# A decoder layer on one core: the first feed-forward turns one gate earlier, the last roots and the fifth weights later

## The chip, the cores and the metric

The kernel runs on one core of a Trainium2 chip. Time is the device time of that core in microseconds; lower is better. A run's time is that of the whole execution; the profile gives, for one profiled execution, the time of every instruction on the five engines: TensorE (PE; its weight loads are PEld), VectorE (DVE), ScalarE (ACT), GpSimd (POOL) and SyncE (SP), which issues most of the DMAs. All data is fp32.

## The reference

Four sequences (B = 4) of 1024 tokens with 512 features go through an attention, a gated convolution over pairs of neighbours, and a quantised feed-forward, each followed by a residual sum and a layer norm:

```python
x = layernorm(x + attention(x))            # 32 heads of 16
x = layernorm(x + xattn(x, ctx, fside))
x = layernorm(x + ffn(x))

def xattn(z1ss, uss, z0, weight, bias):    # h_size 512, kernel 2
    z1h, z1c = z1ss[:, :512], z1ss[:, 512:]
    z0c = concatenate([z0[:, 512:], z1c], axis=2)[:, :, :-1]
    conv = conv1d(concatenate([z0[:, :512], z1h], axis=2), weight)
    it, ot, gt, ft = split(uss + conv + bias, 4, axis=1)
    ct = sigmoid(ft) * z0c + sigmoid(it) * tanh(gt)
    ht = sigmoid(ot) * tanh(ct)
    return concatenate([ht, ct], axis=1)

def ffn(x, ternary_weight, bias, act_scale):
    x_int = clip(round(x / scale), -127, 127)
    return (x_int * scale) @ (ternary_weight - 1).T + bias
```

The convolution's channel axis is the token axis of the layer: rows 0 to 511 of a sequence give `ht` and rows 512 to 1023 give `ct`.

## The kernel before

The attention fills the first 1951 us or so and is not touched. The change lies in `tail`, which does the rest of the layer in two rounds (n = 0 for batches 0 and 2, n = 1 for batches 1 and 3). A round has these stages:

- In round 1 only, the output projection of both batches (`project_out`, lines 772 to 776), eight token tiles each, and the first norm of each batch (`first_norm`, 778 to 785).
- The gates: for each of four blocks t of 128 channels, for each batch of the round, for each of four gates g, one call of `gate` (792 to 819). It does two halves of 16 matmul records (four matmuls for each of two taps): the "ends" into one PSUM tile (`pc`), then the "mids" into another (`pa`). VectorE then adds both to the context with four instructions (lines 806, 809, 810, 812), and ScalarE applies a sigmoid or tanh (813). Both PSUM pools hold two tiles. The taps come from `xf`, which `fir_parts` makes on VectorE from the first norm's output (185 to 191).
- After the fourth gate of a block, `combine` (821 to 858) forms the new state: products on GpSimd (828 to 830), a tanh on ScalarE and sums on GpSimd (833 to 836), statistics on VectorE (841 and 107), the root on ScalarE (117, `deviations`), its reciprocal and the normalisation on VectorE (118 and 121), and a sum on GpSimd (855).
- The feed-forward (`feed_forward`, 914 to 954) over 16 tiles of 128 tokens: `quantise` (864 to 871: one pass on ScalarE, L868, and two on VectorE, L869 and L870), `turn` (873 to 879: four transposes on TensorE, L876, and a copy on ScalarE, L878), `feed` (881 to 885: matmuls, L884), `residual` (887 to 890), and the third norm in groups (`third_norm`, 892 to 908), whose last step, `finish`, writes the tile out.

The order of the tiles in the feed-forward is `order` = 0, 1, 2, 4, 5, 6, 3, 7: tiles 3 and 7 come out of the last block and go last. Tile k + 1 is turned ahead of the matmuls of tile k, and tile k + 3 is quantised behind them.

The program sets the order of instructions by hand (`manual_schedule`): each engine runs its own instructions in the order in which the Python code emits them. `after(n, work)` puts work off by n calls of `step`, one of which follows each gate, each projected tile and each fed tile. So a due number says behind which gate or tile an instruction is emitted, on every engine at once. An instruction that waits holds up all that was emitted behind it on its engine.

Line 983 turns tiles 0 and 1 of the round's first batch between the two halves of the very last gate, and line 987 quantises tiles 0, 1 and 2 in the three gates ahead of it (g = 0, 1, 2 of the second batch at t = 3). The convolution's weights are loaded one block ahead (`load_conv`, 156 to 166, four DMAs of 512 KB; even blocks share one buffer, odd ones another) and their taps summed on GpSimd by `sum_taps` (168 to 170), two instructions each. The weights of the fifth block (m = 4, the first of round 1) are loaded at t = 3 of round 0 (line 989), and summed ahead of the projection (line 969), emitted right behind the feed-forward.

```python
if t == 3 and b == batches[1] and g < 3:
    quantise(batches[0], order[g])
if b == batches[0] and g == 0 and (n, t) != (1, 3):
    w_next = hand.load_conv(4 * n + t + 1, wp)
```

Of the kernel before, what the change touches and what calls it, by code (L numbers as in the profile page):

```python
# [14 lines left out]
P = 128  # L15
B, S, D = 4, 1024, 512
# [3 lines left out]
NT = S // P  # L20
# [718 lines left out]
def tail(ctx, tc, a, out, ident, eps, hand):  # L739
    nc = tc.nc  # L740
# [37 lines left out]
    def first_norm(b):  # L778

        x1[b], parts = hand.first_norm(b)  # L780
        firs[b], more = hand.fir_parts(b, x1[b], hand.shared if b < 2 else fir)
        parts[0]()
        parts[1]()
        for n, part in zip((1, 1, 2, 3, 4, 5) if b == 1 else (1, 1, 2, 2, 3, 3), parts[2:] + more):
            after(n, part)


# [4 lines left out]
    def gate(b, t, g, w, between=None):  # L792
        xf, u = firs[b], us[b, t]
        o = g * P
        ends = ps_c.tile([P, 2, 256], F32, tag="c", name=f"pc{b}_{t}_{g}")
        mids = ps_a.tile([P, 2, 256], F32, tag="a", name=f"pa{b}_{t}_{g}")
        for tap in range(4):
            if tap == 2 and between:
                between()
            pt = (ends, mids)[tap // 2][:, tap % 2, 0:TR]  # L800
            for i in range(FT):
                nc.tensor.matmul(pt, w[:, i, tap, o : o + P], xf[:, tap, i, :], start=i == 0, stop=i == FT - 1)  # L802

        ug = u[:, g, :].rearrange("p (m e) -> p e m", e=3)
        outer = ug[:, 0:3:2, :]
        nc.vector.tensor_add(outer, ends[:, :, 0:TR], outer)
        m, n = (mids[:, i, 0:TR] for i in range(2))
        both = n.unsqueeze(1).to_broadcast([P, 2, TR])
        nc.vector.scalar_tensor_tensor(outer, both, 0.5, outer, ALU.mult, ALU.add)
        nc.vector.scalar_tensor_tensor(ug[:, 1, :], n, -0.5, ug[:, 1, :], ALU.mult, ALU.add)  # L810
        all3 = m.unsqueeze(1).to_broadcast([P, 3, TR])
        nc.vector.scalar_tensor_tensor(ug, all3, 0.5, ug, ALU.mult, ALU.add)  # L812
        nc.scalar.activation(  # L813
            u[:, g, 0:D],
            u[:, g, 0:D],
            AF.Tanh if g == 2 else AF.Sigmoid,
            bias=b_c[:, 4 * g + t : 4 * g + t + 1],
            scale=1.0,
        )

    def combine(b, t, k):


        u, y, x = us[b, t], ys2[b], x1[b]
        ig, og, gg, fg = (u[:, i, 0:D] for i in range(4))
        both = (t, 4 + t)
        made = []
        nc.gpsimd.tensor_mul(gg, ig, gg)
        nc.gpsimd.tensor_mul(fg, fg, x[:, 4 + t, 0:D])
        nc.gpsimd.tensor_add(fg, fg, gg)  # L830

        def second():
            nc.scalar.activation(ig, fg, AF.Tanh)
            nc.gpsimd.tensor_add(y[:, 4 + t, :], fg, x[:, 4 + t, 1 : D + 1])
            nc.gpsimd.tensor_mul(og, og, ig)
            nc.gpsimd.tensor_add(y[:, t, :], og, x[:, t, 1 : D + 1])
            hand.load_ctx(k + 2)

        def third():
            for n, tt in enumerate(both):  # L840
                nc.vector.bn_stats(stats2[b][:, 2 * t + n, :], y[:, tt, :])
            made.append(hand.means(stats2[b], stat, f"2_{b}", 2 * t, 2))

        def fourth():
            made.extend(hand.deviations(made[0], stat, f"2_{b}", 2 * t, 2))

        def fifth():
            mv, rstd, invert = made
            invert()
            for n, tt in enumerate(both):  # L850
                hand.normalised(y[:, tt, :], y[:, tt, :], mv, rstd, 2 * t + n)

        def sixth():
            for tt in both:
                nc.gpsimd.tensor_add(x[:, tt, 0:D], y[:, tt, :], b_f)

        for n, work in ((1, second), (3, third), (4, fourth), (5, fifth), (6, sixth)):
            after(n, work)


# [31 lines left out]
    def third_norm(b, n0, n):  # L892

        y = ys2[b]
        made = []

        def first():
            for m in range(n0, n0 + n):
                halves = 2 if (b, m) == (B - 1, NT - 1) else 1
                nc.vector.bn_aggr(mv3[b][:, m, :], stats3[b][:, m : m + halves, :].rearrange("p h c -> p (h c)"))  # L900
            made.extend(hand.deviations(mv3[b], stat, f"3_{b}", n0, n))

        def finish(m):
            t = order[m]
            hand.normalised(y[:, t, :], y[:, t, :], mv3[b], made[0], m)
            nc.sync.dma_start(out[b, t * P : (t + 1) * P, :], y[:, t, :])

        return first, lambda: made[1](), [lambda m=m: finish(m) for m in range(n0, n0 + n)]

# [2 lines left out]
    mv3 = {}  # L912

    def feed_forward(batches):

        tiles = [(b, n, order[n]) for b in batches for n in range(NT)]
        for b in batches:
            stats3[b] = stat.tile([P, NT + 1, 6], F32, tag="stats3", name=f"stats3_{b}")
            mv3[b] = stat.tile([P, NT, 2], F32, tag="mv3", name=f"mv3_{b}")
        closing = []  # L920
        for k, (b, n, t) in enumerate(tiles):
            end = len(tiles) - k
            if 0 < k < len(tiles) - 1:
                turn(tiles[k + 1][0], tiles[k + 1][2])
            if (b, n) == (B - 1, NT - 1):

                for half in range(2):
                    cols = slice(half * 256, half * 256 + 256)
                    pt = feed(b, t, cols)
                    residual(b, n, t, pt, cols, half)  # L930
            else:
                pt = feed(b, t)
                if k + 3 < len(tiles):
                    quantise(tiles[k + 3][0], tiles[k + 3][2])
                residual(b, n, t, pt)
            for work in closing:
                work()
            closing = []

            last = b == batches[1]  # L940
            group = {5: 2, 6: 1, 7: 1}.get(n, 4 if n == 3 else 0) if last else 4 * (n % 4 == 3)
            if group:
                first, invert, parts = third_norm(b, n + 1 - group, group)
                first()
                if group == 4:
                    after(1, invert)
                    for m, part in enumerate(parts):
                        after(1 + m, part)
                elif group == 2:
                    closing = [invert] + parts  # L950
                else:
                    for work in [invert] + parts:
                        work()
            step()
# [11 lines left out]
    for n, batches in enumerate(((0, 2), (1, 3))):  # L966
        if n:
            for i in range(FT):
                hand.sum_taps(w_next, i)
            for b in batches:  # L970
                if b == 3:
                    after(2, lambda: first_norm(1))
                project_out(b, range(NT))
            first_norm(3)
        for b in batches:
            ys2[b] = hand.tokens(b, f"y2_{b}")
            stats2[b] = stat.tile([P, NT, 6], F32, tag="stats2", name=f"stats2_{b}")
        for t in range(4):
            w = w_next
            for b in batches:  # L980
                for g in range(4):
                    last = (b, t, g) == (batches[1], 3, 3)
                    gate(b, t, g, w, (lambda: [turn(batches[0], order[m]) for m in (0, 1)]) if last else None)
                    if g == 3:
                        combine(b, t, k)
                    if t == 3 and b == batches[1] and g < 3:
                        quantise(batches[0], order[g])
                    if b == batches[0] and g == 0 and (n, t) != (1, 3):
                        w_next = hand.load_conv(4 * n + t + 1, wp)
                        if t < 3:  # L990
                            for i, m in enumerate((3, 6, 6, 7)):
                                after(m, lambda w=w_next, i=i: hand.sum_taps(w, i))
                    step()
                k += 1
        if n == 0:
            big3 = lambda: hand.shared.tile([P, NT * (D + 1)], F32, tag="big0", name="big3")
            after(9, lambda: hand.load_attention(3, big3()))
            after(13, lambda: hand.load_residual(1))
            after(18, lambda: hand.load_residual(3))
        feed_forward(batches)  # L1000
    while later:
        step()

# [40 lines left out]
```

## Time and profile before

| | us |
|---|---|
| runs (3): median, lowest, highest | 2454.65, 2454.08, 2454.93 |
| the profiled execution | 2454.71 |
| its span | 2452.9 |
| TensorE busy | 2431.9 |
| VectorE busy | 1736.9 |
| ScalarE busy | 1337.4 |
| GpSimd busy | 373.7 |
| round 0: gates, feed-forward | from 1951.1, from 2105.2 |
| round 1: projection, gates, feed-forward | from 2171.9, from 2226.9, from 2382.2 |

A row of the timeline gives start, duration, engine, line, operation, output and input with their sizes, and how many instructions are merged (x8 is eight records; a matmul of fp32 data leaves two). In brackets stands how long the engine was idle before it and what ended that. A line of the waits gives who waited for whom, the total, the number of waits and the longest. A row of windows gives the stretch, its length, the busy time, the clock granted to TensorE (1.00 is full speed), the DMA engines' share and GB/s.

### The profile page before, as it was taken

Reading aid. Unit: us, or ns where it says so; the run is one execution under the profiler, and the core shown is the slowest. Engines: PE = TensorE matmul, PEld = TensorE weight load, DVE = VectorE, ACT = ScalarE, POOL = GpSimd, SP = SyncE. Lnnn points to the kernel's source line nnn. Section 1 sums busy time; section 2 is a strip of 40 time slices with the busy share of each in tenths; the row PEclk is TensorE's granted clock in tenths of the full one; section 3 lists DMA queues with packets and bytes.
Section 4 is the critical chain, followed back from the end, with each engine's and each line's share of the span. In section 5 each row is a group of like instructions: output and inputs, shape, how many; then the busy total and the mean of one; then the engine's idle time right before and its main releaser. Section 6 shows DMA issues by size and latency. Waiting matters only on the chain.

```text
span 2452.9 us, 74387 instructions
## 1 busy us (share of the span) xinstructions
PE 2431.9 (99%) x32604; PEld 1691.8 (69%) x32604; DVE 1736.9 (71%) x2180; ACT 1337.4 (55%) x2592; POOL 373.7 (15%) x310
## 2 busy tenths in 40 slices
PE   9999999999999999999999999999999999999998
PEld 5566666666666666666666666666666699548984
DVE  3777777777777777777777777777777476868667
ACT  1166666666666666666666666666655623311332
POOL 2000000000000000000000001000020276502760
PEclk9999999999999999999999999999999999999999
DMA  6101112111111211111111114110120243150311
GB/s 220 50 12 21 21 23 58 22 21 25 22 25 21 53 23 26 21 21 21 21 26 21 22 23 130 26 27 19 25 80 12 85 160 121 52 189 18 121 35 69
DMA packets 80708, 121.70 MB, mean 50 GB/s; under 512 B 39056, under 2 KB 39056, under 8 KB 80384
## 3 DMA queue, kind: packets, MB, share of 16 engines
q1 hardware_dynamic: 79808, 115.90, 16.8%
q8 instruction: 256, 4.19, 0.7%
q10 hardware_dynamic: 576, 1.05, 0.1%
q14 instruction: 68, 0.56, 0.1%
HBM read 80.77 MB, written 18.35 MB: 40 GB/s over the span
## 4 chain that ended last, share of the span: by engine, by line
PE 97%; DVE 2%; ACT 1%; issue 0%; DVEq 0%
PE nat L457 22%; PE av L553 20%; PE st L527 18%; PE proj L59 10%; PE pa L802 5%; PE pc L802 5%; PE v L59 5%; PE pf L884 4%; PE po L59 2%; PE po L237 2%; PE fold L361 1%; PE fold L59 1%; PE tr L876 0%; DVE xq L869 0%; DVE y L121 0%; DVE xq L870 0%
## 5 line engine op out<-in xcount | busy, mean ns | idle before, releaser
L473 DVE TENSOR_REDUCE mx<-nat 128x2 f32<-128x1024 f32 x1008 | 1187.7, 1219 | 439.7 <-PE st L527 412.1
L538 ACT ACTIVATE at<-st 128x512 f32<-128x512 f32 x2016 | 1042.3, 603 | 608.1 <-PE st L527 595.6
L457 PE MATMUL nat<-qk 32*128 32x512 f32 x4032 | 1012.2, 614 | 0.5 <-DVE mx L473 0.5
L527 PE MATMUL st<-qk 32*128 32x256 f32 x8064 | 998.0, 387 | 0.0
L527 PEld LDWEIGHTS st<-qk 32*128 32x128 f32 x8064 | 662.2, 184 | 46.1 <-issue 3.7
L553 PE MATMUL av<-at,v_sb 128*32 128x256 f32 x8192 | 498.5, 382 | 1.5 <-ACT at L538 1.5
L457 PEld LDWEIGHTS nat<-qk 32*128 32x128 f32 x4032 | 343.2, 184 | 188.3 <-DVE mx L473 119.7
L553 PEld LDWEIGHTS av<-at,v_sb 128*32 128x32 f32 x8192 | 241.0, 109 | 223.6 <-ACT at L538 92.3
L600 POOL TENSOR_TENSOR o_n<-o_sb,rbc 128x512 f32<-128x512 f32 x64 | 98.1, 1555 | 1673.2 <-DMA rbc<-rec_d 1619.1
L59 PE MATMUL proj<-xT,w_qk 128*32 128x176 f32 (+1 forms) x6144 | 259.4, 311 | 0.7 <-ACT w_qk L366 0.7
L59 PEld LDWEIGHTS proj<-xT,w_qk 128*32 128x32 f32 x6144 | 181.3, 109 | 82.0 <-ACT at L538 60.0
L802 PE MATMUL pc<-xf,w 128*128 128x171 f32 x1024 | 160.0, 308 | 1.6 <-DVE xf L191 1.0
L802 PE MATMUL pa<-xf,w 128*128 128x171 f32 x1024 | 159.8, 308 | 0.0
L802 PEld LDWEIGHTS pc<-xf,w 128*128 128x128 f32 x1024 | 152.0, 189 | 2.8 <-DVE xf L191 1.2
L802 PEld LDWEIGHTS pa<-xf,w 128*128 128x128 f32 x1024 | 152.0, 189 | 0.0
L813 ACT ACTIVATE u<-u,b_c 128x512 f32<-128x512 f32 x64 | 46.3, 723 | 163.6 <-DVE u L812 163.6
L884 PE MATMUL pf<-w_f,xq_t 128*128 128x512 f32 (+1 forms) x264 | 120.8, 604 | 7.6 <-ACT xq_t L878 7.6
L59 PE MATMUL v<-w_v,xT 128*32 128x256 f32 x2048 | 122.5, 382 | 0.0
L566 DVE TENSOR_TENSOR o_sb<-av,o_sb 128x256 f32<-128x256 f32 x128 | 54.3, 424 | 72.0 <-PE av L553 71.4
L59 PEld LDWEIGHTS v<-w_v,xT 128*32 128x32 f32 x2048 | 60.6, 109 | 58.1 <-ACT at L538 16.6
L170 POOL TENSOR_TENSOR w<-w 128x512 f32<-128x512 f32 x64 | 80.5, 1292 | 110.5 <-DMA w<-in_conv_wT 110.5
L564 ACT COPY o_sb<-av 128x256 f32<-128x256 f32 x128 | 48.0, 375 | 77.9 <-PE av L553 59.3
(99 smaller groups left out, 1321.7 us busy)
## 6 DMA issues: line engine op xcount, KB each, us to landing
qk<-qk SPq DMA_DIRECT2D x256, 64.0 KB
w<-in_conv_wT SPq DMA_DIRECT2D x32, 512.0 KB
u<-in_ctx SPq DMA_DIRECT2D x16, 1024.0 KB
xT<-in_xT SPq DMA_DIRECT2D x16, 512.0 KB
rbc<-rec_d SPq DMA_DIRECT2D x128, 64.0 KB
attn<-o_n SPq DMA_DIRECT2D x256, 32.0 KB
big<-attn SPq DMA_DIRECT2D x4, 2048.0 KB
y<-in_x SPq DMA_DIRECT2D x4, 2048.0 KB
```

Of the source, the lines that this page charges most:

```text
L59: nc.tensor.matmul(pt[r, :], lhsT(f)[:, r], rhs(f), start=f == 0, stop=f == FT - 1)
L170: self.nc.gpsimd.tensor_tensor(w[:, i, tap, :], w[:, i, 0, :], w[:, i, 1, :], op)
L237: nc.tensor.matmul(pt, attn_t[:, f, t * P : (t + 1) * P], self.w_o[:, f, cols], start=f == 0, stop=f == FT - 1)
L457: nc.tensor.matmul(pts[n], q_ts[u % 4][r : r + 32, qt * P : (qt + 1) * P], k_ts[u % 4][r : r + 32, kh * 512 : kh * 512 + 512], start=True, ...
L473: nc.vector.tensor_reduce(mxs[u][:, qt, 2 * pair : 2 * pair + 2, kh], pt, AX.X, ALU.max, negate=True)
L527: nc.tensor.matmul(st[:, k * QW : k * QW + QW], k_ts[u % 4][r : r + 32, kt * P : (kt + 1) * P], q_ts[u % 4][r : r + 32, qq * QW : qq * QW ...
L538: nc.scalar.activation(at, st, AF.Exp, scale=0.25)
L553: nc.tensor.matmul(av[32 * j : 32 * j + 32, :], v_sb[b % 2][:, kt, c * VW : c * VW + 32], ats[u, 2 * i + n // 2, j][:, n % 2 * QW : n % 2 ...
L566: nc.vector.tensor_add(o, av, o)
L600: nc.gpsimd.tensor_mul(o_n[:, :, half * 256 : half * 256 + 256], o_sb[:, cols].rearrange("p (s e) -> p e s", e=2), rbc[:, cols].rearrange( ...
L802: nc.tensor.matmul(pt, w[:, i, tap, o : o + P], xf[:, tap, i, :], start=i == 0, stop=i == FT - 1)
L884: nc.tensor.matmul(pt, xq_ts[b, t][:, f, :], hand.w_f[:, f, cols], start=f == 0, stop=f == FT - 1)
```

## The change

Five things are done.

- `quantise` of tiles 0, 1, 2 moves one gate earlier: to the last gate of the first batch and the first two of the second ("place" 3, 4, 5). The turn of tiles 0 and 1 moves from the last gate to the one ahead of it ("place" 6), again between its halves.
- `combine`'s root, normalisation and bias sum of the last block (t = 3) are due two steps later.
- In the feed-forward, a group's first step (its aggregate and root) is emitted ahead of what the group before has left over, and the very last tile is normalised and written in two halves, the second DMA from ScalarE's queue.
- `first_norm` emits the two parts of the FIR (the making of `xf`) ahead of the normalisation of tiles 4 to 7, which `xf` does not read.
- The fifth block's weights are loaded behind the first feed-forward (behind its output DMAs on SP's queue), and their taps summed in the projection, at steps 3 to 6.

The diff, cut to what matters:

```diff
@@ first_norm
-        for n, part in zip((1, 1, 2, 3, 4, 5) if b == 1 else (1, 1, 2, 2, 3, 3), parts[2:] + more):
+        for n, part in zip((1, 1, 2, 3, 4, 5) if b == 1 else (1, 1, 2, 3, 4, 4), parts[2:4] + more + parts[4:]):
             after(n, part)
@@ combine
-        for n, work in ((1, second), (3, third), (4, fourth), (5, fifth), (6, sixth)):
+        late = 2 * (t == 3)
+        for n, work in ((1, second), (3, third), (4 + late, fourth), (5 + late, fifth), (6 + late, sixth)):
             after(n, work)
@@ third_norm
         def finish(m):
             t = order[m]
-            hand.normalised(y[:, t, :], y[:, t, :], mv3[b], made[0], m)
-            nc.sync.dma_start(out[b, t * P : (t + 1) * P, :], y[:, t, :])
+            n = 2 if (b, m) == (B - 1, NT - 1) else 1
+            for h in range(n):
+                part = y[:, t, h * D // n : (h + 1) * D // n]
+                hand.normalised(part, part, mv3[b], made[0], m)
+                (nc.scalar if h else nc.sync).dma_start(
+                    out[b, t * P : (t + 1) * P, h * D // n : (h + 1) * D // n], part
+                )
@@ feed_forward
-            for work in closing:
-                work()
-            closing = []
...
                 first()
+            for work in closing:
+                work()
+            closing = []
+            if group:
@@ tail
         if n:
             for i in range(FT):
-                hand.sum_taps(w_next, i)
+                after(3 + i, lambda i=i: hand.sum_taps(w_next, i))
...
                 for g in range(4):
-                    last = (b, t, g) == (batches[1], 3, 3)
-                    gate(b, t, g, w, (lambda: [turn(batches[0], order[m]) for m in (0, 1)]) if last else None)
+                    place = 4 * (b == batches[1]) + g if t == 3 else 0
+                    gate(b, t, g, w, (lambda: [turn(batches[0], order[m]) for m in (0, 1)]) if place == 6 else None)
                     if g == 3:
                         combine(b, t, k)
-                    if t == 3 and b == batches[1] and g < 3:
-                        quantise(batches[0], order[g])
-                    if b == batches[0] and g == 0 and (n, t) != (1, 3):
+                    if place in (3, 4, 5):
+                        quantise(batches[0], order[place - 3])
+                    if b == batches[0] and g == 0 and t < 3:
                         w_next = hand.load_conv(4 * n + t + 1, wp)
...
         feed_forward(batches)
+        w_next = hand.load_conv(4, wp) if n == 0 else None
```

No arithmetic is added or left out. Each round has two fewer loads of ScalarE's function table, since the root of batch 0's or 1's last block no longer stands between two sigmoids.

More of the change, by code (lines that the diff above doesn't have):

```diff
@@ L981, in tail @@
                 for g in range(4):
-                    last = (b, t, g) == (batches[1], 3, 3)
-                    gate(b, t, g, w, (lambda: [turn(batches[0], order[m]) for m in (0, 1)]) if last else None)
+                    place = 4 * (b == batches[1]) + g if t == 3 else 0
+                    gate(b, t, g, w, (lambda: [turn(batches[0], order[m]) for m in (0, 1)]) if place == 6 else None)
                     if g == 3:
                         combine(b, t, k)
-                    if t == 3 and b == batches[1] and g < 3:
-                        quantise(batches[0], order[g])
-                    if b == batches[0] and g == 0 and (n, t) != (1, 3):
+                    if place in (3, 4, 5):
+                        quantise(batches[0], order[place - 3])
+                    if b == batches[0] and g == 0 and t < 3:
                         w_next = hand.load_conv(4 * n + t + 1, wp)
-                        if t < 3:
-                            for i, m in enumerate((3, 6, 6, 7)):
-                                after(m, lambda w=w_next, i=i: hand.sum_taps(w, i))
+                        for i, m in enumerate((3, 6, 6, 7)):
+                            after(m, lambda w=w_next, i=i: hand.sum_taps(w, i))
                     step()
```

## The prediction, made before the changed kernel was run

> **What bounds the kernel now.** The page comes first. TensorE is busy 99% of the span, and the chain that ended last lies on it:
>
> ```profile
> PE 97%; DVE 2%; ACT 1%; issue 0%; DVEq 0%
> ```
>
> An edit that adds no TensorE work and takes none away can therefore gain only where TensorE stands still or runs slowly. The page's other engines (DVE 71%, ACT 55%) matter only through the waits they end. So I next asked for the waits in the stretch that the diff touches, from 2060 us to the end:
>
> ```profile
> PE pf L884 <- ACT xq_t L878: 7.6, 3, 3.7
> PE tr L876 <- DVE xq L870: 1.3, 2, 1.0
> PE pc L802 <- DVE xf L191: 1.0, 1, 1.0
> ```
>
> These are totals, counts and the longest wait. Two of the three waits of the first line are the 3.7 us ones, one at the start of each feed-forward. The timeline of TensorE shows what follows the first:
>
> ```profile
> 2105.23 6.57 PE L884 MATMUL pf<-w_f,xq_t 128*128 128x512 f32 x8 [3.70 <-ACT xq_t L878]
> 2111.64 0.60 PE L876 MATMUL tr<-ident,xq 128*128 128x128 f32 x4
> 2112.07 3.60 PE L884 MATMUL pf<-w_f,xq_t 128*128 128x512 f32 x8
> 2115.51 0.60 PE L876 MATMUL tr<-ident,xq 128*128 128x128 f32 x4
> ```
>
> The reader is to see two things. The first tile took 6.57 us where an undisturbed one takes 3.44 (3.60 with its pipelined end). And the turn of the fourth tile (tile 4, "tr_4" below) began at 2115.51 right behind other work. The windows of half a microsecond give the reason for the first, the granted clock (last columns but two):
>
> ```profile
> 2103.50:2104.00 0.50, 0.00 (x0) 1.00 0.00 0
> 2104.00:2104.50 0.50, 0.00 (x0) 0.72 0.00 0
> 2104.50:2105.00 0.50, 0.00 (x0) 0.50 0.00 0
> ...
> 2111.00:2111.50 0.50, 0.50 (x2) 0.95 0.00 0
> ```
>
> The clock halves 2.7 us into the idle time and stays so for 6.8 us. So a stall of 3.70 us costs 3.70 + 3.13 = 6.8 us. In the second feed-forward the windows show the same: idle from 2378.5, half clock from 2380.7 to 2387.5, and a first tile of 6.35 us, so 3.70 + 2.91 = 6.6 us. That is the largest prize. The next question is what else is close behind. VectorE's timeline answers it:
>
> ```profile
> 2105.93 0.85 DVE L812 SCALAR_TENSOR_TENSOR u<-pa,u 128x513 f32<-128x513 f32 x1
> 2106.70 0.14 DVE L118 RECIPROCAL rstd<-rstd 128x2 f32<-128x2 f32 x1
> 2106.88 1.00 DVE L121 TENSOR_SCALAR y<-y,mv,rstd 128x512 f32<-128x512 f32 x2
> 2111.78 1.27 DVE L869 TENSOR_SCALAR xq<-xq 128x512 f32<-128x512 f32 x1 [3.90 <-ACT xq L868]
> 2113.09 1.37 DVE L870 TENSOR_SCALAR xq<-xq,sc 128x512 f32<-128x512 f32 x1
> ```
>
> The last two rows quantise tile 4. They end at 2114.46, and tr_4 began at 2115.51: **only 1.05 us of slack** behind a TensorE that was 6.8 us late. In the second stage they end at 2391.39 and tr_4 begins at 2392.21: 0.8 us.
>
> **Part 1: turning tiles 0 and 1 one gate earlier, quantising 0, 1, 2 one gate earlier.** No instruction is added. The copies (L878) now stand on ScalarE ahead of the last two sigmoids and behind xq_2 alone, no longer behind a table load (1.28) and a root (0.29). I follow VectorE, whose order decides, from the end of gate (b0, g3) at 2083.85:
> - xq_0: its ScalarE pass starts 0.62 after that gate's sigmoid (2083.88) and takes 0.80, to 2085.3. Then two passes on VectorE. GpSimd is busy from 2084.68 to 2091.2, and beside GpSimd L869 and L870 take 1.39 and 1.37 (row 2090.08) instead of 0.43 and 0.49 (row 2096.84): 2088.1.
> - The root's reciprocal and two L121 now fall into the busy stretch too. Before they took 1.00 together at 2083.95; one beside GpSimd took 1.29 (row 2126.36). Bounds 1.0 and 2.6; I take 2.6, the row with the same neighbour: 2090.7.
> - Gate g0's four instructions 2.5 (2104.28 to 2106.78): 2093.2. Idle 1.49 until ScalarE's xq_1, then 0.9: 2095.6.
> - g1 2.5, idle 1.5, xq_2 0.9, stats 1.4 (L841, L107), g2 and g3 5.0: 2106.9. Before: 2106.78. What is saved, 1.2 us of waiting for TensorE before g0, is eaten by the slower L121.
>
> TensorE beside it: the first half of g2 ends at 2093.7, the turns need xq_1 at 2095.6 and wait about 1.5 us (new, everything of TensorE queued behind), then three half gates of 2.33 and 0.5 of turn: 2103.25. The copies are made by 2100.6, so the wait at the first tile is gone. Tile 0, turn 2, tile 1: 3.44 + 0.43 + 3.44, to 2110.6. Now tr_4 needs xq_4. That pass sits on ScalarE behind the tanh (L833), which waits for GpSimd, which waits for the last sigmoid, which waits for g3 on VectorE: 7.7 us from g3's end (2106.78) to L870's end (2114.46) before, unchanged. So tr_4 starts at 2106.9 + 7.7 = 2114.5: **the stall moves from the first tile to tr_4 and is 3.9 us long.** TensorE has reached tr_4 only 1.0 us earlier than before (0.8 in the second stage), and it has gone idle once more.
>
> **Does the clock fall again?** The rows: idle 2.7 and 2.2 us was enough, and 6.8 us at half clock followed, 3.0 us lost on average. The Trainium skill, "TensorE: Matmul & The Clock Gate", section "What's actually happening", speaks of a free-running window of about 3.4 us, idle to throttle and busy to release. By it a restart that fills its first window is at half clock for 3.4 us only, a loss of 1.7. The rows show 6.8 us twice, but both restarts fell inside a window. Sum for two stages by the rows 6.0, by the rule 3.4. The phase of the window is not mine to know: 2.6 each, nearer to the rows. For no loss at all the idle would have to be split so that neither window notices; a wait of 1.03 us before the turn at 2136.07 left the clock at 1.00, so one of about 1 us is harmless.
>
> Stage 1: -1.0 + 2.6 = +1.6. Stage 2: -0.8 + 2.6 = +1.8.
>
> **Part 2: fifth weights behind the outputs.** Four 512 KB issues (2.51 us of SP's queue at 2073.01) move behind the last output at about 2176, and GpSimd's eight sums (10.94 us from 2128.75) from inside the first feed-forward into the projection. There they slowed L121, L869 and L870 to 1.4 each. TensorE's twelve tile periods from tr_4 to the last turn take 46.47 us in the second feed-forward (2392.21 to 2438.68) and 49.11 in the first (2115.51 to 2164.62). The difference, **-2.64 us**, is gained. Behind the four issues on SP stand the residual (2 MB, needed by L242 at 2200.9) and the sixth weights. Two loads of 2 MB took from 2177.8 to 2190.9 before; three, begun at 2176, are done near 2193 at the measured 390 GB/s. The sums end by about 2203 and are needed at 2226.9. Hidden by 24 us; L242 goes from 0.68 to 1.53 beside them (row 2190.62), inside VectorE's 1.42 us of idle per tile. If the cover went, each late microsecond would cost one.
>
> **Part 3: first norm's taps before its last tiles.** Four L121 (1.91) leave the path to L191, which TensorE waits for at 2247.82. The break between its two halves there is 2247.82 - 2246.72 = 1.1 us. Next in line is L189/L191 beside GpSimd's product at 2243.7, at worst done at 2245.8 where 2246.7 is asked: **-1.1**.
>
> **Part 4: the end.** The root of the next-to-last tile no longer waits 0.36 us on VectorE, and the last 0.55 us pass and 256 KB output are halved on two queues. Bounds 0 and -1.0; I take **-0.6**. The roots moved behind (L121 of the last tiles) have about 10 us until they are read: nothing.
>
> Sum: +1.6 + 1.8 - 2.64 - 1.1 - 0.6 = -0.9. The profiled execution took 2454.71 us (span 2452.9, 1.8 around it), 0.06 above the median of three, 2454.65. **2453.8 us.** A measurement of this kernel tells no change within 0.2%, 4.9 us.
>
> **Rivals.**
> - *The clock holds in both new stalls.* For it: the phase may split 3.9 us into two harmless pieces. Against: one piece is always at least 1.95 us, and 2.2 was enough. -0.9 - 5.2 = -6.1: 2448.6.
> - *The stall goes and nothing takes its place.* Then 3.7 + 3.1, 3.7 + 2.9, 2.64, 1.1 and 0.6 are all gained, 17.7 us: 2437.0. For it: the waits name L878 alone. Against: xq_4 would have to be there by 2109, 5 us earlier. A shorter backlog (L121 at 1.0, so 1.6 earlier per stage) gives part of it: 2450.6, or 2445.4 with a warm clock.
> - *Slower: VectorE's backlog grows.* Quantising and roots both lie beside GpSimd from 2084.7 to 2091.2. If they hold up GpSimd and g0 too, say by 2.0 us, tr_4 is 2.0 later in both stages: +4.0 - 0.9 = +3.1, 2457.8. It decides from 0.45 us of further delay per stage. Against: g0's PSUM instructions ran at full speed beside GpSimd at 2086.7.
>
> **Chances.** Forecast 0.60, clock holds 0.14, stall goes wholly or largely 0.18, backlog grows 0.08. Faster by over 0.2% takes the second (most) and the third and a sliver of the first: 0.32. Slower by over 0.2% is half of the fourth: 0.04. Within: 0.64. The range goes from a shortened backlog with a clock that holds nearly throughout, 2446.5, to the grown backlog, 2457.5; the likeliest case alone has 2451.5 to 2456.
>
> **What would show it.** Right: no wait at the first tile, a wait of about 1.5 us before the turns in the gate, and one of some 3.9 us of tr_4 for xq (L870) in each feed-forward, clock 0.50 behind it; no long L121 after 2127; no wait for L191. Wrong: tr_4 without a wait, or a clock of 1.00 throughout.

## The result and the profile after

The changed kernel takes 2452.47 us in the median of 20 runs (2450.55 to 2453.91), the kernel before 2454.92 in 20 runs beside it (2453.75 to 2456.37). The ratio is 0.9989, with a 95% interval of 0.9982 to 0.9996: 2.45 us less, and less than 0.2%. The profiled execution took 2451.39 us, with a span of 2449.6.

The view of the waits of TensorE, from 2060 us to the end, shows what became of the three lines of before. One line is left (total, number, longest):

```profile
PE tr L879 <- DVE xq L873: 10.1, 4, 3.9
```

L879 and L873 are the old L876 (turn) and L870 (quantise). The waits for the copy and for `xf` are gone. Four waits for a quantised tile stand in their place, two in each round. TensorE's timeline of round 0 shows where (start, duration, engine, line, operation; in brackets the idle time before):

```profile
2096.15 0.66 PE L879 MATMUL tr<-ident,xq 128*128 128x128 f32 x4 [1.16 <-DVE xq L873]
...
2103.65 3.59 PE L887 MATMUL pf<-w_f,xq_t 128*128 128x512 f32 x8
...
2107.52 3.60 PE L887 MATMUL pf<-w_f,xq_t 128*128 128x512 f32 x8
2114.97 1.09 PE L879 MATMUL tr<-ident,xq 128*128 128x128 f32 x4 [3.85 <-DVE xq L873]
2115.85 4.51 PE L887 MATMUL pf<-w_f,xq_t 128*128 128x512 f32 x8
```

The first two tiles run back to back at full speed. The turn of the fourth tile, tr_4, then waits 3.85 us (3.86 in round 1), where the first tile used to wait 3.70. The windows of half a microsecond give the granted clock (third figure from the right):

```profile
2114.00:2114.50 0.50, 0.00 (x0) 0.76 0.00 0
2114.50:2115.00 0.50, 0.03 (x1) 0.50 0.00 0
...
2117.50:2118.00 0.50, 0.50 (x2) 0.83 1.02 389
```

The reader should see that the clock falls again, but for 3.4 us only, where it was 6.8 before. In round 1 it is the same, 3.4 us from 2387.33. VectorE's timeline gives the steps of the backlog that the prediction had followed:

```profile
2086.23 0.90 DVE L872 TENSOR_SCALAR xq<-xq 128x512 f32<-128x512 f32 x1 [1.49 <-ACT xq L871]
...
2088.65 2.53 DVE L121 TENSOR_SCALAR y<-y,mv,rstd 128x512 f32<-128x512 f32 x2
...
2106.46 0.85 DVE L813 SCALAR_TENSOR_TENSOR u<-pa,u 128x513 f32<-128x513 f32 x1
2112.16 1.27 DVE L872 TENSOR_SCALAR xq<-xq 128x512 f32<-128x512 f32 x1 [4.84 <-ACT xq L871]
2113.46 1.36 DVE L873 TENSOR_SCALAR xq<-xq,sc 128x512 f32<-128x512 f32 x1
```

The two L121 take 2.53 us together, where they took 1.00; the last gate ends at 2107.31; tile 4 is quantised at 2114.82, and tr_4 starts at once.

Set against the trace of before, with common points of TensorE's timeline as marks, the 3.3 us by which the span is shorter divide as follows. ("The pa half" is the second half of a gate, into the PSUM tile `pa`. Half clock costs half of the time at work under it: in round 0 TensorE works from 2114.97 to the release at 2117.67, 2.70 us, and loses 1.35.)

| stretch of the span | forecast | measured |
|---|---|---|
| up to the pa half at 2079.49 (after: 2080.39) | 0 | +0.90 |
| from there to tr_4 of round 0 | -1.0 | -1.44 |
| tr_4 to the last turn of round 0 (49.11 to 47.82) | +2.6 - 2.64 | -1.29 |
| round 1 up to the pa half at 2249.09 (after: 2246.03) | -1.1 | -1.23 |
| from there to tr_4 of round 1 | -0.8 | -1.18 |
| tr_4 to the last turn of round 1 (46.47 to 47.86) | +2.6 | +1.39 |
| the last turn to the end of the span | -0.6 | -0.45 |
| sum | -0.94 | -3.30 |

The +0.90 of the first row lies ahead of every instruction of a compute engine that the change moves. Where it comes from is told at the end.

### The profile page after: what moved, and what is told of

It is laid out like the page before. It is cut to its first block, busy times and chain, and to the rows that moved or that the text cites. A ratio compares the mean times of both kernels' runs of the same rounds, so it can differ in the third digit from the quotient of the medians.

```text
span 2449.6 us, 74384 instructions
## 1 busy us (share of the span) xinstructions
PE 2428.4 (99%) x32604; PEld 1691.0 (69%) x32604; DVE 1736.5 (71%) x2181; ACT 1332.3 (54%) x2588; POOL 373.7 (15%) x310
## 3 DMA queue, kind: packets, MB, share of 16 engines
q10 hardware_dynamic: 720, 1.18, 0.1%
## 4 chain that ended last, share of the span: by engine, by line
PE 96%; DVE 2%; ACT 1%; issue 0%; POOL 0%; DMA 0%; SPq 0%; DVEq 0%; ACTq 0%
PE nat L457 22%; PE av L553 20%; PE st L527 18%; PE proj L59 10%; PE pc L803 5%; PE pa L803 5%; PE v L59 5%; PE pf L887 4%; PE po L59 2%; PE po L237 2%; PE fold L361 1%; PE fold L59 1%; PE tr L879 1%; DVE u L813 0%; DVE xq L873 0%
```

## The experiments

Each kernel ran beside the kernel before on the same chip. The medians:

| kernel | median us (runs) | before, same chip | difference | ratio, 95% interval |
|---|---|---|---|---|
| the change | 2452.47 (20) | 2454.92 | -2.45 | 0.9989 [0.9982, 0.9996] |
| turns alone | 2458.22 (21) | 2455.23 | +2.99 | 1.0012 [1.0006, 1.0019] |
| weights as before | 2455.96 (13) | 2455.23 | +0.73 | 1.0005 [0.9997, 1.0013] |
| taps and end as before | 2454.53 (13) | 2454.84 | -0.31 | 0.9999 [0.9991, 1.0007] |
| roots as before | 2455.33 (13) | 2454.84 | +0.49 | 1.0001 [0.9992, 1.0009] |
| before, filled wait | 2454.92 (13) | 2454.84 | +0.08 | 0.9999 [0.9991, 1.0007] |
| the change, filled wait | 2449.48 (11) | 2455.23 | -5.75 | 0.9977 [0.9969, 0.9986] |
| split passes | 2443.25 (5) | 2455.23 | -11.98 | 0.9955 [0.9943, 0.9968] |
| and residual first | 2440.78 (5) | 2454.84 | -14.06 | 0.9943 [0.9930, 0.9957] |
| and roots later still | 2439.33 (5) | 2455.36 | -16.03 | 0.9932 [0.9918, 0.9945] |

A comparison of two variants below is one of their differences to before. The interval of one difference is about 2 us to either side, and 3 us for the three kernels with five runs, so what lies closer together is told apart by the traces alone.

### The turns alone

Parts 2 to 4 of the prediction (weights, taps, end) are undone; the earlier turns and quantising and the later roots stay. The pieces of `third_norm` and `feed_forward`, undone as well, are not in this excerpt:

```diff
-        for n, part in zip((1, 1, 2, 3, 4, 5) if b == 1 else (1, 1, 2, 3, 4, 4), parts[2:4] + more + parts[4:]):
+        for n, part in zip((1, 1, 2, 3, 4, 5) if b == 1 else (1, 1, 2, 2, 3, 3), parts[2:] + more):
...
-                after(3 + i, lambda i=i: hand.sum_taps(w_next, i))
+                hand.sum_taps(w_next, i)
...
-                    if b == batches[0] and g == 0 and t < 3:
+                    if b == batches[0] and g == 0 and (n, t) != (1, 3):
                         w_next = hand.load_conv(4 * n + t + 1, wp)
...
-        w_next = hand.load_conv(4, wp) if n == 0 else None
```

> Only the earlier turn, the earlier quantising and the later roots; weights, taps and end as before. Theory A (the wait is moved, not removed): no wait at the first tile, about 1.2 us before the second turn in the gate and 3.9 us before the turn of the fourth tile in both feed-forwards, each with a clock drop; against the kernel before, 0 to +2 us (2455 to 2457). Theory B (the earlier turn is what made the kernel faster): at least half of the 2.45 us, 2453.7 or less.

The time is 2.99 us above that of before, 1 us more than the 0 to 2 expected: the change's main part, alone, is a loss. Its waits are those of the full change (1.21 us in the gate, 3.88 and 3.84 at tr_4), with those for the fifth weights' sums and for `xf` besides. This is near the working of part 1 (+1.6 and +1.8 are +3.4). A stall that had gone without a successor would have gained several microseconds.

The trace shows one thing that the change's own does not. In round 1 the same stall at tr_4 is followed by 6.8 us at half clock (2390.82 to 2397.64), not by 3.4. TensorE's two rows behind the stall, and the window in which the clock comes back:

```profile
2392.15 1.09 PE L879 MATMUL tr<-ident,xq 128*128 128x128 f32 x4 [3.84 <-DVE xq L873]
2393.03 5.89 PE L887 MATMUL pf<-w_f,xq_t 128*128 128x512 f32 x8
```

```profile
2397.50:2398.00 0.50, 0.50 (x3) 0.85 0.00 0
```

From tr_4 to the last turn it takes 49.21 us, 2.7 more than the 46.47 of the kernel before. That is the 2.6 of the prediction, where the change itself has 1.4.

### The weights as before

Only part 2 is undone (the last three pieces of the diff above).

> The changed kernel with the fifth weights loaded and summed where they were before. Theory A: the first feed-forward gets back the slow VectorE passes beside GpSimd's sums, 2.6 us, so about 2455.1, the same as the kernel before, while the second feed-forward, the taps and the end stay as in the changed kernel. Theory B: well under 1 us more than the changed kernel, 2452.5 to 2453.5.

This is 3.2 us more than the change. The trace of TensorE shows two waits in the middle of the first feed-forward:

```profile
2145.61 0.63 PE L879 MATMUL tr<-ident,xq 128*128 128x128 f32 x4 [0.76 <-DVE xq L873]
2147.93 3.70 PE L887 MATMUL pf<-w_f,xq_t 128*128 128x512 f32 x8 [1.69 <-ACT xq_t L881]
```

They are 2.45 us, and the clock stays at full speed behind each. Beside GpSimd's sums (11.05 us from 2138.28) L872 and L873 take 1.48 and 1.37 us, and 0.42 and 0.49 in the changed kernel at that place, until TensorE runs dry. The later loads hurt nothing: in the changed kernel no wait of TensorE stands in the projection. From tr_4 to the last turn of round 0 it takes 51.09 us here and 47.82 in the changed kernel. These 3.27 us are more than the 2.64 forecast: in the kernel before, the sums began about 10 us earlier (2128.75), and the three waits in that stretch were 1.57 us together.

### The taps and the end as before

Parts 3 and 4 are undone.

> The changed kernel with the taps and the end of the feed-forward as before. Theory A: the wait for the taps (1.0 to 1.2 us) comes back once, and 0.4 us at the end: 2454.0 to 2454.3. A rival, that these two gave nothing and the whole gain is the weights': 2452.5.

This is 2.1 us more than the change. The view of TensorE's waits has one line more than that of the changed kernel:

```profile
PE pc L803 <- DVE xf L191: 1.0, 1, 1.0
```

The changed kernel's trace against that of before has 1.23 us at the taps and 0.45 at the end, 1.7 together as forecast. Not all of the 2.1 us need be theirs. In this run's trace the clock stays at half for 6.8 us in round 1 (2386.80 to 2393.62), which makes that feed-forward 1.2 us longer than in the change; and its gates began 1.0 us earlier (1950.14 against 1951.14), which no edit explains.

The three parts add up: +3.0 - 3.2 - 2.1 = -2.3, where -2.45 was measured. With intervals of 2 us on each, so close a sum is in part luck.

### The roots as before

```diff
-        late = 2 * (t == 3)
+        late = 0
```

> The changed kernel with the roots of the last block's tiles at their old steps, so that two table loads and a root stand again between the last two sigmoids on ScalarE. By the prediction's word (they have time until they are read) nothing: 2452.5. Theory A, corrected: they delay the last sigmoid by about 1.2 us, and with it the tanh and the fourth tile's turn, in both rounds, and lengthen the stall: 2454.8 to 2456.5.

This is 2.9 us more than the change. ScalarE's timeline shows the cause:

```profile
2103.85 0.72 ACT L814 ACTIVATE u<-u,b_c 128x512 f32<-128x512 f32 x1 [3.88 <-DVE u L813]
2104.59 1.28 ACT L117 ACT_TABLE_LOAD   x1
2105.89 0.30 ACT L117 ACTIVATE rstd<-mv,eps 128x2 f32<-128x2 f32 x1
2106.20 1.28 ACT L814 ACT_TABLE_LOAD   x1
2107.49 0.72 ACT L814 ACTIVATE u<-u,b_c 128x512 f32<-128x512 f32 x1
```

The root of the first batch's last block needs another function table than the sigmoids on both sides of it. VectorE had ended the last gate at 2106.28, but its sigmoid starts at 2107.49, behind the second load. From that sigmoid on the tanh, tile 4's pass and tr_4 follow, and tr_4 waits 5.01 us in each round instead of 3.85. So moving the roots is worth 1.16 us a round. In this trace the clock adds 1.4 us in round 0, where it stays at half for 6.8 us (2113.77 to 2120.59), and 0.1 in round 1, where it stays for 3.4.

### A filled wait, in the kernel before and after

Four matmuls, whose result is overwritten, are put into the stall, so that TensorE is busy when it would idle. In the kernel before they stand in `feed`, ahead of the first tile of a round; in the changed one in `turn`, ahead of tr_4. The edit to the one and then to the other, in excerpts:

```diff
+        for f in range(4 * warm):
+            nc.tensor.matmul(pt, hand.w_f[:, f, 0:P], hand.w_f[:, f, :], start=True, stop=True)
...
-                pt = feed(b, t)
+                pt = feed(b, t, warm=k == 0)
```

```diff
+        if (b % 4 < 2) and t == order[3]:
+            for f in range(4):
+                nc.tensor.matmul(
+                    tr.rearrange("p f o -> p (f o)"), hand.w_f[:, f, 0:P], hand.w_f[:, f, :], start=True, stop=True
+                )
```

> The kernel before, with four matmuls of a tile's size (3.4 us, result overwritten) put where TensorE waits 3.70 us ahead of the first tile. The clock stays up and the first tile takes 3.44. Theory A (only 1.05 and 0.8 us of slack at the fourth tile's turn): a new wait of about 2 us stands there in both rounds, and of the 6.0 us only 1.9 are gained, less if the clock drops in the new wait: 2453 to 2455.5. If the first tile's wait and clock are what the end hangs on: 6 us, 2449.

> The changed kernel with four matmuls of the fourth tile's size (3.4 us) whose result is overwritten, put where TensorE waits 3.85 us for that tile. Theory A: the turn starts where it did, the clock stays at 1.00, and only the loss to the half clock goes: 2.8 us in the profile (1.4 in each feed-forward), 3 to 5 in the median, so 2447.5 to 2449.5. If the loss is not the clock's (slow turn by another cause): no gain. If the filler is in the way: slower than 2452.5.

In the kernel before, TensorE's timeline shows the first tile free of its cold clock, and the same stretch waiting further on:

```profile
2101.75 3.59 PE L884 MATMUL pf<-w_f 128*128 128x512 f32 x8
2105.64 3.70 PE L886 MATMUL pf<-w_f,xq_t 128*128 128x512 f32 x8 [0.30 <-ACT xq_t L878]
...
2115.02 0.63 PE L876 MATMUL tr<-ident,xq 128*128 128x128 f32 x4 [1.80 <-DVE xq L870]
```

The clock loss at the first tile, close to 3 us in each round, is taken away, and the time does not move (+0.08, with an interval of 2 us to either side, where the rival had 6 us less). tr_4 starts when tile 4 is quantised, 0.9 and 0.65 us earlier than before, counted from the last half gate. This is the plainest evidence for the prediction's reading: behind the stall of before, close to 7 us with its clock, there was about 1 us to be had, whatever is done about the first tile.

In the changed kernel the same filler gains 3.3 us:

```profile
2110.30 3.60 PE L880 MATMUL tr<-w_f 128*128 128x512 f32 x8
2114.26 0.66 PE L884 MATMUL tr<-ident,xq 128*128 128x128 f32 x4 [0.36 <-DVE xq L873]
2114.95 3.67 PE L892 MATMUL pf<-w_f,xq_t 128*128 128x512 f32 x8
```

tr_4 still starts when its tile is there. Only the cold clock is gone (the turn 0.66 instead of 1.09, the tile 3.67 instead of 4.51). By the medians the clock loss behind the new stalls was 1.65 us each, with 1.4 us of doubt to either side. The traces have less: from tr_4 to the last turn it takes 46.87 us in both rounds here, and 47.82 and 47.86 in the changed kernel, 1.0 each. The two profiled executions differ by 2.77 us, as expected, but 0.7 of that lies ahead of the gates, which begin at 1950.46 here and at 1951.14 there.

### The fourth tile brought forward too

If tr_4 waits for tile 4, tile 4 must come earlier as well. The pass on ScalarE is put between the two halves of a gate, ahead of that gate's sigmoid; the passes on VectorE go behind the gate; tile 4 is done like the first three, in the gate ahead of the last; and the feed quantises four tiles ahead. In the excerpt of the edit to the changed kernel, `scaled` is the pass on ScalarE and `rounded` the two on VectorE, together the old `quantise`:

```diff
+                    def between():
+                        scaled(batches[0], order[place - 3])
+                        if place == 6:
+                            for m in (0, 1):
+                                turn(batches[0], order[m])
-                    gate(b, t, g, w, (lambda: [turn(batches[0], order[m]) for m in (0, 1)]) if place == 6 else None)
+                    gate(b, t, g, w, between if place in (3, 4, 5, 6) else None)
...
-                    if place in (3, 4, 5):
-                        quantise(batches[0], order[place - 3])
+                    if place in (3, 4, 5, 6):
+                        rounded(batches[0], order[place - 3])
...
-                if k + 3 < len(tiles):
-                    quantise(tiles[k + 3][0], tiles[k + 3][2])
+                if k + 4 < len(tiles):
+                    quantise(tiles[k + 4][0], tiles[k + 4][2])
                 residual(b, n, t, pt)
```

> The changed kernel with quantising split: ScalarE's pass of tiles 0, 1, 2 and 4 is issued between the halves of the gate, ahead of that gate's sigmoid, VectorE's passes behind the gate's four instructions; tile 4 is so quantised ahead of the last gate and not behind the tanh. Theory A: the three idle times of 1.49 us on VectorE go, the wait before the second turn (1.16) and the one before the fourth tile's (3.85) with its clock loss (1.4 and more) go, in both rounds: 12 to 14 us, 2438.5 to 2440.5. A rival, that VectorE as a whole is late there: a wait of 2 to 4 us stays at the turn of the fifth or sixth tile, 2446 or more.

The time falls by 9.5 us against the change, but 2443.25 misses the 2438.5 to 2440.5 expected. Both kinds of wait are gone, but a new one is there in each round (2.36 and 2.38 us), at a place that the rival did not name either. One row on TensorE and one chain on VectorE show it:

```profile
2112.34 5.37 PE L891 MATMUL pf<-w_f,xq_t 128*128 128x512 f32 x8 [2.36 <-DVE y L896]
```

```profile
2108.92 1.28 DVE L873 TENSOR_SCALAR xq<-xq 128x512 f32<-128x512 f32 x1 [4.84 <-ACT xq L869]
2110.23 1.36 DVE L874 TENSOR_SCALAR xq<-xq,sc 128x512 f32<-128x512 f32 x1
2111.52 0.68 DVE L896 TENSOR_TENSOR y<-pf,big 128x512 f32<-128x512 f32 x1
```

L896 is the residual of the first tile. It reads the PSUM tile that the third tile's matmuls are to fill. It stands on VectorE behind the quantising of the fifth tile, which waits 4.84 us for ScalarE. That is a wait of order alone: the sum had been ready since the first tile's matmuls ended. So the edit after it swaps the two:

```diff
                 pt = feed(b, t)
+                residual(b, n, t, pt)
                 if k + 4 < len(tiles):
                     quantise(tiles[k + 4][0], tiles[k + 4][2])
-                residual(b, n, t, pt)
```

> As split_all, with the residual of a fed tile issued ahead of the quantising of the tile four places on (split_all left a wait of 2.36 us at the third tile's matmuls for a PSUM tile whose reader stood on VectorE behind the fifth tile's quantising). Theory A: that wait goes, and with it 1.8 us of half clock, in both rounds; the fifth tile is quantised by 2111.6 and turned at 2113.3 at the earliest, so nothing is late next: 7 to 8 us less than split_all, 2435 to 2437. A rival, that VectorE is late by then: a wait of 2 us or more at a later turn, 2440 or more.

It misses the expectation: 2440.78, where at most 2437 was expected. The wait for PSUM is gone and the clock is at 1.00 in both feed-forwards up to their last turns. But the expectation had taken its 1.8 us of half clock from the profiled execution of the split version, which was 3.0 us above the median of that kernel, and a second wait had stood right behind the first:

```profile
2111.53 3.70 PE L891 MATMUL pf<-w_f,xq_t 128*128 128x512 f32 x8 [1.05 <-ACT xq_t L885]
```

The third tile's copy stands on ScalarE behind the fifth tile's pass, a table load (2109.42, 1.28 us) and the root. The wait is 2.1 us for both rounds. Here the root is in the way once more, so it goes one fed tile further, with the normalisation left in its place:

```diff
-        late = 2 * (t == 3)
-        for n, work in ((1, second), (3, third), (4 + late, fourth), (5 + late, fifth), (6 + late, sixth)):
+        ahead, behind = (7, 7) if t == 3 else (4, 5)
+        for n, work in ((1, second), (3, third), (ahead, fourth), (behind, fifth), (behind + 1, sixth)):
```

> Split passes and residual first, with the last blocks' roots and their table load one fed tile later on ScalarE (the normalisation stays in its place on VectorE). The one wait left on TensorE in each feed-forward, 1.05 us of the third tile for its copy, stood behind a table load (1.28) and a root (0.29). Theory A (the copy goes behind the quantising pass alone, at 2109.4 by the trace, and is done at 2110.0 where TensorE asks at 2110.3): no wait of TensorE above 0.1 us from the gates to the end, 2.1 us less than before this edit, about 2438.7 us. Theory B (the load now delays the fourth tile's copy or the reciprocal on VectorE, and the wait comes back one tile later): a wait of 0.5 to 1 us at the fourth or fifth tile, 2440 to 2441.

The time is 2.0 us less than that of the version before it, where 2.1 was expected; with five runs of each, the medians alone would not tell. The traces have 0.85 us less in each round from the last half gate to the last turn. ScalarE and then TensorE in this kernel:

```profile
2109.56 0.56 ACT L885 COPY xq_t<-tr 128x512 f32<-128x512 f32 x1
...
2110.86 1.28 ACT L117 ACT_TABLE_LOAD   x1
```

```profile
2110.13 0.60 PE L883 MATMUL tr<-ident,xq 128*128 128x128 f32 x4
2110.57 3.60 PE L891 MATMUL pf<-w_f,xq_t 128*128 128x512 f32 x8
```

The copy is made ahead of the load, and the tile follows its turn with no wait; two waits of 0.2 us are all that TensorE has left from 2060 us to the end. This version is the fastest of the study, 13.6 us ahead of the change.

## Why the prediction came out as it did

**The stall moves: right.** "The stall moves from the first tile to tr_4 and is 3.9 us long": 3.85 and 3.86. The wait in the gate was put at about 1.5 us and is 1.16 and 1.19. The rows behind it hold: two L121 at 2.6 (2.53), the last gate's end at 2106.9 (2107.31, in a trace that is 0.9 late by then), tr_4 at 2114.5 (2114.97). That TensorE could only gain what slack stood behind the old stall was put at 1.0 and 0.8 us; it is 1.44 and 1.18, as VectorE's chain came out about 0.4 us shorter than the working had it. The filled wait in the kernel before shows that this slack, and not the stall's length, was the prize. One of the signs, "no long L121 after 2127", failed: three L121 at 2133.53 take 2.41 us, beside the bias sum that the late roots have moved there. TensorE waits for none of them.

**The clock's price: the term that was mis-sized, by luck of the phase.** The prediction took 2.6 us for each new stall, "nearer to the rows" (3.0) than to the Trainium skill's rule (1.7). The rows themselves were read 0.16 too high: the 6.57 and 6.35 us of the first tiles hold the pipelined end, which the 3.44 leave out. From the first tile's start to the next turn it is 6.41 and 6.18 us, so the clock took 2.97 and 2.74. The change's trace has 1.35 and 1.39. But 2.6 was not too much for every stall: five kernels here leave the stall at tr_4 unfilled, and in three of their ten the clock stayed at half for 6.8 us and cost 2.6 to 2.7 (turns alone and taps and end as before in round 1, roots as before in round 0). In the other seven it stayed for 3.4.

In the Trainium skill, "TensorE: Matmul & The Clock Gate", section "What's actually happening", the window is free-running and 3413 ns long. The traces agree. The clock fell at 2104.22 and 2380.70 in the trace of before, 276.48 us apart, and at 2114.26 and 2387.33 after, 273.07 apart: 81.0 and 80.0 times 3.413. It stayed low for 6.83 us before and for 3.41 after, two windows and one. What decides between the two, in these traces, is how much of the first slow window TensorE filled after its restart. Where it filled 70% or less (70% and 57% before, 51% to 61% in the three long stalls above), the clock was released one window later; where it filled 79% or more (79% and 81% after, 88% or more elsewhere), at once. So the change's two stalls, at 79% and 81%, came out on the cheap side by little, and the prediction, which said that it did not know the phase, could not have known this. Executions differ too: four of the change's 20 runs have a mean granted clock of 0.997 where the others have 0.998, and they are 1.4 us longer on average. That fits one long stall in place of a short one; their windows were not recorded.

**The weights: right in kind.** -2.64 was forecast, and the change's trace gives the whole of it (47.82 us less a clock loss of 1.35 is 46.47 again). Undone in the changed kernel, it is 3.2 by the medians and 3.27 by the trace, as the sums then stand at a worse place.

**The taps and the end: right.** -1.7 forecast, -1.68 in the trace, -2.1 in the median, part of which may be the clock's.

**"The roots moved behind ... nothing": a step that left out the gain.** Late roots cost nothing, as said. But the move itself takes two table loads and a root from ahead of the last sigmoid, worth 1.16 us a round in the new order. The sum of part 1 was made in the new order, so the total holds this gain without having named it. Had the turns been moved without the roots, that sum would have been 2.3 us too low.

**The rivals.** A clock that holds was given 2448.6; the filled wait, which forces it, has 2449.48. That the stall goes wholly was given 2437.0; the last version, which does what the change does not (tile 4 early, the PSUM reader and the copy ahead of what waits), has 2439.33. So both prices were about right, and neither came about in the change. The slower rival, a grown backlog, didn't come: the last gate ended when it was said to.

The forecast sum of -0.9 and the measured -2.45 differ by 1.5 us, and in the two traces, -3.30, by 2.4. There the clock's term accounts for 2.5 (5.2 forecast, 2.74 measured) and the larger slack for 0.8; the +0.90 of the first stretch takes it back. That the gain came out larger than forecast is thus luck of the phase in good part: with two long stalls, 5.2 us in place of 2.74, the change's trace would, by this estimate, be 0.8 us ahead of that of before and not 3.3.

## What to carry to other kernels

Before you remove a wait of the bounding engine, work out when the next operand on that engine will be there: the gain is the slack behind the stall, and the rest comes back as a wait one or two instructions on. Where the engines run in order, the late operand is often ready in substance and only stands behind something that waits (a residual behind a quantising pass, a copy behind a table load); swapping the two cost nothing here. A stall can cost more than its length: in these traces waits of up to 1.8 us left the clock at full speed, and those of 2.36 us and more, where nothing filled them, were each followed by 3.4 or 6.8 us at half clock.

## What the runs showed of the hardware that was not expected

**How little idle time the clock notices.** Waits of 1.80 and 1.82 us left it at 1.00 (the filled wait before). In the split version TensorE was idle for 2.36 us and had been at work again for 1.2 when the clock halved; windows of that kernel:

```profile
2112.50:2113.00 0.50, 0.50 (x2) 1.00 0.52 111
2113.00:2113.50 0.50, 0.50 (x3) 1.00 0.91 270
2113.50:2114.00 0.50, 0.50 (x2) 0.51 0.98 369
```

The drop is at 2113.51, and the next one of this trace is 269.65 us later, 79.0 times 3.413, so it comes at a window's end. That window began at 2110.10 and was idle until 2112.34: TensorE was busy for 34% of it. So a window need not be wholly idle. That execution was the slowest of its five (2446.24, median 2443.25), with a mean clock of 0.998 where the other four had 0.999, so the same wait may well have cost the others less; their windows were not recorded.

**Half a microsecond by who starts first.** The +0.90 of the first stretch is mostly one wait of 0.55 us in the fourth gate of round 0 (g = 3 of its first batch), which the change doesn't touch. The timeline of the kernel before, and then of the changed one, at the same place:

```profile
1960.63 5.02 POOL L600 TENSOR_TENSOR o_n<-o_sb,rbc 128x512 f32<-128x512 f32 x2 [27.89 <-DMA rbc<-rec_d]
1960.66 1.12 DVE L185 TENSOR_TENSOR xf<-big 128x684 f32<-128x684 f32 x1
```

```profile
1960.60 3.83 POOL L600 TENSOR_TENSOR o_n<-o_sb,rbc 128x512 f32<-128x512 f32 x2 [27.79 <-DMA rbc<-rec_d]
1960.75 2.31 DVE L185 TENSOR_TENSOR xf<-big 128x684 f32<-128x684 f32 x1
```

GpSimd's product and VectorE's sum begin within 0.15 us of each other. In seven of the eleven profiles GpSimd is 0.11 to 0.16 us ahead, takes 3.8 us for its two products, and VectorE's sum takes 2.3. In the other four (the kernel before, roots as before, the filled wait before, the split passes) VectorE begins between 0.11 us ahead and 0.03 behind, its sum takes 1.1 us, and GpSimd's two products 4.9 to 5.0. The Trainium skill, "SBUF — State Buffer", section "SBUF: two separate sides", has the two engines take a shared port as an exclusive lock, first come first served, where VectorE reads two operands from SBUF, as here. These rows fit that, as far as starts on GpSimd can be read to 0.03 us. The wait and the refill behind it are 0.8 us of a single profile. Another stretch of luck lies ahead of it: the gates begin between 1950.14 and 1951.92 us in the eleven profiles, though no edit touches the attention. A comparison of single profiles by their span says nothing at that size; one from mark to mark, as in the table above, leaves this out.
